# A decoder layer on one core: two transposes moved from TensorE to block-moving DMAs and VectorE

## The chip, the cores and the metric

The kernel runs on one core of a Trainium2 chip. The core has five engines that run side by side, each with its own queue of instructions in a fixed order: TensorE (PE, matrix products), VectorE (DVE), ScalarE (ACT), GpSimd (POOL) and SyncE (SP), which here only issues DMAs. Sixteen DMA engines move the data. PE writes to PSUM, which has eight banks; everything else lies in SBUF, in 128 partitions. The metric is the device time of one execution in microseconds (us), the median of several runs.

## The reference

For four batch entries of 512 rows and 512 columns (f32) it computes a pre-norm decoder layer: causal self-attention with 16 heads of 32 columns, causal cross-attention in which the context serves as keys and as values without any weights, and a feed-forward part with a gated expert. Every part is preceded by a layer norm and added to x.

```python
x = x + attn(_layernorm(x), q_w, q_b, k_w, k_b, v_w, v_b, o_w, o_b)   # softmax(q k^T / sqrt(32)), causal
x = x + _mha(_layernorm(x), ctx_2048, ctx_2048)                       # the same, k = v = context
x = x + ffn(_layernorm(x), W_up, W_down, W_gate, W_expert)            # relu(f Wup) Wdown + sum(rw) * (f Wexpert)
```

In the cross-attention masked scores are set to -10000 and not to minus infinity.

## The kernel before

**Tiling.** The rows of one entry are split into four tiles of 128 rows (`NT`), the columns into four blocks of 128 (`NC`), and a block of 128 columns holds four heads (`HG`). A tensor is kept either by rows (128 rows on the partitions) or turned, with the columns on the partitions: `[128, 4, 512]`, block by row. A projection contracts over columns, so it needs its input turned. This holds for the normalised x of every norm and for the context, which the cross-attention needs both by rows (`cv`, the values) and turned (`ck_t`, the keys).

**How turning is done.** The helper `columns` (line 255) has PE transpose eight 128x128 blocks into a PSUM pair, that is two banks (line 259), and ACT copy the pair to SBUF (line 265, or with a factor at line 267).

**Stages.** The loop at line 1033 goes over the four entries b. Per entry: `with_maxima` runs the score products whose row maxima the softmax needs, with other matmuls between them; `attend` runs the products again, the exponentials and the products with the values; `out_projection` (line 739) multiplies by the output weights; then the norm before the cross-attention, turned by `norm_cross` (line 766, tile `tp_q`); then `with_maxima`, `attend` and `add_cross` for the cross-attention; then the norm, turned by `norm_ffn`, and the feed-forward part. Parts of the feed-forward and of the next entry's projections serve as filling in the `with_maxima` stages.

**What runs ahead.** The next entry's first norm is made inside the current entry's self-attention `with_maxima` (`norm_in(b + 1)`, line 604): tiles `xin` are loaded, and `xn_a` are the normalised tiles, four of them. Its `turns` and those of the context (`context`, line 714) are run by `out_projection` as `sides`, between the groups of matmuls: after the first group the first two tiles of the context and one half of x, after the second group the other half of the context, after the third the other half of x. After the second group stand also the suffix sums of the context on DVE, `behT` (`behind`, line 725, four scans at line 730). At its end the sums `pm_o` are added to x on DVE (line 760), each tile's statistics are taken, and the norm `xn_q` is made (line 216).

**After the output projection** PE's order is: two steps of filling (line 1047; the next entry's query and key projection, `pm_qk`, from `xnT`; in the last entry the gate product and one step of the up projection), then the transposes of `xn_q` tiles 0 and 1 (`tp_q`), one more step, and those of tiles 2 and 3.

**What sets the order.** PE, DVE, ACT and POOL run in the order in which the program issues (`BY_HAND`, line 17). SP's order is set by a scheduler. The framework gives DMAs eight completion lanes in turn, so a DMA is issued only once the eighth before it has landed. Tiles of one tag share a buffer, and a new tile waits until all readers of the old one are done. `xn_t` has one buffer: the turned x of the next entry may be written only after the value projection `pm_v` of the current one, which reads it. For entry 0 that projection stands in the self-attention `with_maxima`; for the later ones it was done in the entry before. The tags `ck_t` and `beh_t` also hold the sums of exponentials of the self-attention's head groups (line 432): group 1 has `beh_t`, groups 0 and 2 have `ck_t`. The sums of group 1 are last read by PE at line 562, the second of three such groups of matmuls in the stage.

Of the kernel before, what the change touches and what calls it, by code (L numbers as in the profile page):

```python
# [9 lines left out]
F32 = mybir.dt.float32  # L10
# [8 lines left out]
P = 128  # L19
# [7 lines left out]
def decoder_layer(  # L27
# [21 lines left out]
    nc = tc.nc  # L49
    B, S, D = x.shape  # L50
    NH = 16
    HD = D // NH
    NT = S // P
    NC = D // P
    HG = P // HD
# [4 lines left out]
    act = ctx.enter_context(tc.tile_pool(name="act", bufs=1))  # L60
# [4 lines left out]
    def pair(name):  # L65

        return ps.tile([P, 2, S], F32, tag="ps", name=name)
# [78 lines left out]
    for r in range(HG):  # L146
# [23 lines left out]
        out=nfloor,  # L170
        in_=nfloor,
# [8 lines left out]
    for n in range(2):  # L180
        t = const.tile([P, NT, P], BF16, name=f"parts{n}")
# [3 lines left out]
    def keep_warm(name, count):  # L185

        out = pair(name)
        for n in range(count):
            nc.tensor.matmul(
                out[:, 0, :P], lhsT=ident, rhs=ident, start=True, stop=True  # L190
            )
# [63 lines left out]
    def columns(srcs, dst, t, tp, scale=None):  # L255

        for n, src in enumerate(srcs):
            for c in range(NC):
                nc.tensor.transpose(
                    tp[:, n, c * P : (c + 1) * P], src[:, c * P : (c + 1) * P], ident  # L260
                )
        to = dst[:, :, t * P : (t + 2) * P].rearrange("p c (n q) -> p c n q", q=P)
        come = tp.rearrange("p n (c q) -> p c n q", q=P)
        if scale is None:
            nc.scalar.copy(to, come)
        else:
            nc.scalar.mul(to, come, scale)
# [336 lines left out]
    def norm_in(b, given=None):  # L604

        e = Entry()
        e.b, e.x, e.xn_t = b, given, None
        src = x[b].rearrange("(t p) d -> p t d", p=P)

        def source(t):  # L610
            if given is not None:
                return given[:, t, :]
            xi = work.tile([P, D], F32, tag="xin", name=f"xin_{b}_{t}")
            nc.sync.dma_start(out=xi, in_=src[:, t, :])
            return xi

        made, norms = layernorms(source, f"a{b}", ahead=given is not None)
        if given is not None:
            norms = [norms[n] for n in (0, 1, NT, NT + 1, 2, 3, NT + 2, NT + 3)]

        def turn(t):
            if e.xn_t is None:
                e.xn_t = act.tile([P, NC, S], F32, tag="xn_t", name=f"xnT_{b}")
            columns(
                [made[t], made[t + 1]],
                e.xn_t,
                t,
                pair(f"tp_a{b}_{t}"),
            )

        def turn_one(t):
            if t == 0:
                e.xn_t = act.tile([P, NC, S], F32, tag="xn_t", name=f"xnT_{b}")
            tp = pair(f"tp_a{b}_{t}")[:, 0, :]
            for c in range(NC):
                cols = slice(c * P, (c + 1) * P)
                nc.tensor.transpose(tp[:, cols], made[t][:, cols], ident)
            nc.scalar.copy(
                e.xn_t[:, :, t * P : (t + 1) * P], tp.rearrange("p (c q) -> p c q", q=P)
            )  # L640

        if given is not None:
            return e, norms, [(lambda t=t: turn_one(t)) for t in range(NT)]
        return e, norms, [(lambda t=t: turn(t)) for t in (0, 2)]

    def add_bias(e):
        for t in range(NT):
            nc.gpsimd.tensor_tensor(e.x[:, t, :], e.x[:, t, :], bo_sb, ALU.add)
# [65 lines left out]
    def context(e):  # L714

        b = e.b
        e.cv = cvs.pop(b)
        e.ck_t = act.tile([P, NC, S], F32, tag="ck_t", name=f"ckT_{b}")

        def one(t):  # L720
            columns([e.cv[:, t, :], e.cv[:, t + 1, :]], e.ck_t, t, pair(f"tp_c{b}_{t}"))

        return [(lambda t=t: one(t)) for t in (0, 2)]

    def behind(e, c):

        if c == 0:
            e.beh_t = act.tile([P, NC, S], F32, tag="beh_t", name=f"behT_{e.b}")
        nc.gpsimd.memset(e.beh_t[:, c, S - 1 : S], 0.0)
        nc.vector.tensor_tensor_scan(  # L730
            e.beh_t[:, c, S - 2 :: -1],
            e.ck_t[:, c, S - 1 : 0 : -1],
            zero.to_broadcast([P, S - 1]),
            0.0,
            ALU.add,
            ALU.add,
        )

    def out_projection(e, a, sides):

        b = e.b
        pms = [pair(f"pm_o{b}_{n}") for n in range(2)]
        for c in range(NC):
            for t in range(NT):
                nc.tensor.matmul(  # L745
                    pms[t // 2][:, t % 2, :],
                    lhsT=a.out[:, c, t * P : (t + 1) * P],
                    rhs=wo_sb[:, c, :],
                    start=(c == 0),
                    stop=(c == NC - 1),  # L750
                )
            if c < NC - 1:
                run(sides[c::3])
            if c == 1:
                for g in range(NC):
                    behind(e, g)

        def add(t):
            xi = e.x[:, t, :]
            nc.vector.tensor_tensor(xi, pms[t // 2][:, t % 2, :], xi, ALU.add)  # L760

        made, norms = layernorms(lambda t: e.x[:, t, :], f"q{b}", add)
        run(norms)
        return made
# [149 lines left out]
    def run(steps):  # L914
        for step in steps:
            for _ in step() or ():
                pass
# [101 lines left out]

    with tc.manual_schedule(engines=BY_HAND):  # L1020
        e, norms, turns = norm_in(0, x0)
        keep_warm("warm", 12)
        between_self = query_key(e) + value(e)
        run(norms[:4] + turns[:2] + between_self[:1])
        run(norms[4:] + turns[2:])
        nc.gpsimd.tensor_scalar(bqs_sb, bq_sb, SCALE, None, ALU.mult)
        nc.vector.tensor_reduce(
            fold, ident.rearrange("p (c e) -> p e c", e=HD), axis=AX.X, op=ALU.add
        )
        add_bias(e)  # L1030
        between_self = between_self[1:]
        skip, between_cross, ahead = 6, [], []
        for b in range(B):
            more = b + 1 < B
            sa = Attention(e.q_t, e.k_t, e.v, False, f"s{b}")
            norms, turns = [], []
            if more:
                after, norms, turns = norm_in(b + 1)
            late = with_maxima(between_self, sa, skip, norms)
            if b == B - 1:  # L1040
                e.x = load_x(b)
            attend(sa, late)
            if b > 0:
                add_bias(e)
            made = out_projection(e, sa, context(e) + turns)
            steps = (query_key(after) if more else []) + between_cross
            run(steps[:2])
            norm_cross(e, made, 0)
            run(steps[2:3])
            norm_cross(e, made, 2)  # L1050
            ca = Attention(e.cq_t, e.ck_t, e.cv, True, f"c{b}")
            ca.e, ca.out = e, e.beh_t
            late = with_maxima(steps[3:], ca)
            if b + 2 < B:
                after.x = load_x(b + 1)
            attend(ca, late)
            if more:
                cvs[b + 1] = load_cv(b + 1)
            filler = value(after) if more else ahead
            run(filler[:1])  # L1060
            made = add_cross(e, ca)

            fill = matmuls(filler[1:])
            for t, k in ((0, 8), (2, 2)) if b != B - 2 else ((0, 12), (2, 0)):
                for _ in range(k):
                    next(fill)
                norm_ffn(e, made, t)
            for _ in fill:
                pass
            gates, ups, downs, experts = ffn(e)  # L1070
            if b + 3 < B:
                between_self, between_cross = gates[:1] + ups + gates[1:] + downs, experts
            elif b + 2 < B:
                between_self, between_cross = gates[:1] + ups + gates[1:] + downs, []
                ahead = experts
            elif more:
                between_self, ahead = ahead + ups[:2], experts
                between_cross = gates[:1] + ups[2:] + gates[1:] + downs
            else:
                run(gates[:1] + ups + gates[1:])  # L1080
                run(downs[:2] + experts[:2] + downs[2:] + experts[2:])
            skip = 0
            if more:
                e = after
# [48 lines left out]
```

## Time and profile before

| | |
|---|---|
| Median of 3 runs | 802.95 us (802.95 to 803.22) |
| Profiled execution's own time | 803.28 us |
| Its span, first to last instruction | 801.5 us |
| PE busy | 794.1 us (99%) |
| DVE busy | 566.4 us (71%) |
| ACT busy | 395.4 us (49%) |
| POOL busy | 340.0 us (42%) |
| DMA packets | 16337, of them 2064 under 512 B |
| TensorE clock granted | 1.0 throughout |

The profiled execution is 0.33 us above the median, and 1.8 us of it lie outside the span. Busy is the time in which an engine had at least one instruction in work. Matmuls overlap: the duration of one (272 ns for a 128x128 f32 transpose) runs from its start to its result, while the next may start long before. What a matmul costs PE is the distance to the next one's start. One 128x512 f32 matmul appears as two instructions.

### The profile page before, as it was taken

To read this page: it belongs to the slowest core of one execution; us is meant where nothing else is said; L and a number is where in the kernel's file an instruction comes from. 1 tells how busy PE (TensorE), PEld (TensorE's weight loads), DVE (VectorE), ACT (ScalarE), POOL (GpSimd) and SP (SyncE) were. 2 spreads that over 40 slices of the span, in tenths; PEclk is the share of its full clock that TensorE was granted. 3 is DMA by queue.
4 is the path that set the end of the run, shared out by engine and by line. 5 is a ranking of instruction groups with operands and counts; after the bars stand their busy time and mean duration, and the time that the engine had idled before them with its cause. 6 is when DMAs were issued, how large, how long until landed. Compare 5 with 4: busy or idle time off the path is not lost.

```text
span 801.5 us, 13955 instructions
## 1 busy us (share of the span) xinstructions
PE 794.1 (99%) x5600; PEld 379.5 (47%) x5600; DVE 566.4 (71%) x963; ACT 395.4 (49%) x450; POOL 340.0 (42%) x523
## 2 busy tenths in 40 slices
PE   8999999999999999999999999999999999999998
PEld 7444554445444454444544445444444454444444
DVE  2478866888678854588867786688859766988512
ACT  2557426871547515666045752687056824674110
POOL 3435612664234732267233482266423653475100
PEclk9999999999999999999999999999999999999999
DMA  9700000001000000021100000000102000000101
GB/s 311 266 28 1 2 1 1 2 28 54 1 27 1 2 1 0 2 80 53 53 14 14 1 2 1 0 1 2 54 28 80 2 2 0 1 2 2 52 1 52
DMA packets 16337, 24.51 MB, mean 31 GB/s; under 512 B 2064, under 2 KB 6416, under 8 KB 16272
## 3 DMA queue, kind: packets, MB, share of 16 engines
q1 hardware_dynamic: 15552, 22.96, 8.3%
q8 instruction: 44, 0.72, 0.4%
q10 hardware_dynamic: 720, 0.66, 0.2%
q14 instruction: 21, 0.17, 0.1%
HBM read 19.42 MB, written 4.19 MB: 29 GB/s over the span
## 4 chain that ended last, share of the span: by engine, by line
PE 96%; ACT 2%; issue 1%; DVE 0%; POOL 0%; POOLq 0%
PE pm_qk L245 13%; PE pm_d L233 7%; PE pm_u L245 7%; PE pm_v L233 7%; PE pm_o L745 7%; PE pm_e L233 7%; PE pv_c L486 6%; PE pv_s L486 6%; PE sm_c L297 6%; PE sm_s L297 6%; PE sc_s L409 5%; PE sc_c L409 5%; PE sc_s L420 1%; PE sc_c L420 1%; PE pv_s L562 1%
## 5 line engine op out<-in xcount | busy, mean ns | idle before, releaser
L328 DVE TENSOR_REDUCE nm_s<-s_s 128x2 f32<-128x1024 f32 (+3 forms) x128 | 96.9, 810 | 31.0 <-POOL s_s L316 30.9
L328 DVE TENSOR_REDUCE nm_c<-s_c 128x2 f32<-128x1024 f32 (+3 forms) x128 | 95.9, 811 | 31.0 <-POOL s_c L316 31.0
L308 ACT COPY s_s<-sm_s 128x1024 f32<-128x1024 f32 x80 | 77.1, 1015 | 70.7 <-PE sm_s L297 36.4
L308 ACT COPY s_c<-sm_c 128x1024 f32<-128x1024 f32 x80 | 77.1, 1016 | 35.9 <-PE sm_c L297 16.2
L316 POOL TENSOR_SCALAR_AFFINE_SELECT s_c<-s_c 128x512 f32<-128x512 f32 (+1 forms) x80 | 44.1, 552 | 100.2 <-ACT s_c L308 100.2
L316 POOL TENSOR_SCALAR_AFFINE_SELECT s_s<-s_s 128x512 f32<-128x512 f32 (+1 forms) x80 | 44.0, 554 | 92.9 <-ACT s_s L308 92.9
L556 DVE TENSOR_TENSOR sum_s<-sum_s,pt_s 128x256 f32<-128x256 f32 (+2 forms) x72 | 60.0, 898 | 15.4 <-PE pv_s L486 15.4
L443 ACT ACTIVATE pt_c<-sc_c 128x1024 f32<-128x1024 f32 x64 | 61.7, 1031 | 18.4 <-PE sc_c L420 10.1
L233 PE MATMUL pm_d<-wdown_sb,hT 128*128 128x512 f32 x128 | 61.5, 610 | 0.0
L451 POOL TENSOR_SCALAR_AFFINE_SELECT pt_c<-pt_c 128x512 f32<-128x512 f32 (+1 forms) x64 | 52.5, 828 | 21.1 <-ACT pt_c L443 20.7
L245 PE MATMUL pm_u<-fT,wup_sb 128*128 128x512 f32 x128 | 59.3, 604 | 0.0
L443 ACT ACTIVATE pt_s<-sc_s 128x1024 f32<-128x1024 f32 x56 | 53.9, 1029 | 10.5 <-POOL pt_s L451 5.5
L233 PE MATMUL pm_v<-wv_sb,xnT 128*128 128x512 f32 x128 | 58.8, 600 | 0.0
L745 PE MATMUL pm_o<-wo_sb,oT_s 128*128 128x512 f32 x128 | 57.8, 596 | 0.0
L409 PE MATMUL sc_c<-cqT,ckT 32*128 32x384 f32 (+3 forms) x512 | 56.4, 464 | 0.9 <-ACT sum_c L443 0.9
L245 PE MATMUL pm_qk<-xnT,wk_sb 128*128 128x512 f32 x120 | 57.3, 607 | 0.0
L245 PE MATMUL pm_qk<-xnT,wq_sb 128*128 128x512 f32 x120 | 56.7, 604 | 0.0
L233 PE MATMUL pm_e<-wexp_sb,fT 128*128 128x512 f32 x120 | 56.3, 604 | 0.0
L451 POOL TENSOR_SCALAR_AFFINE_SELECT pt_s<-pt_s 128x512 f32<-128x512 f32 (+1 forms) x56 | 48.0, 867 | 16.8 <-ACT pt_s L443 16.2
L409 PE MATMUL sc_s<-qT,kT 32*128 32x128 f32 (+3 forms) x512 | 54.0, 464 | 0.9 <-ACT sum_s L443 0.9
L297 PE MATMUL sm_c<-ckT,cqT 32*128 32x512 f32 (+3 forms) x512 | 47.5, 460 | 0.0
L297 PE MATMUL sm_s<-kT,qT 32*128 32x512 f32 (+3 forms) x512 | 47.0, 461 | 0.0
(177 smaller groups left out, 1274.8 us busy)
## 6 DMA issues: line engine op xcount, KB each, us to landing
cv<-in_ctx_dram SPq DMA_DIRECT2D x16, 256.0 KB, 3.7
out_dram<-x SPq DMA_DIRECT2D x15, 256.0 KB, 2.1
xin<-in_x_dram SPq DMA_DIRECT2D x12, 256.0 KB, 2.6
x<-in_x_dram SPq DMA_DIRECT2D x12, 256.0 KB, 4.0
wv_sb<-in_wv_dram SPq DMA_DIRECT2D x1, 1024.0 KB, 8.3
wo_sb<-in_wo_dram SPq DMA_DIRECT2D x1, 1024.0 KB, 9.9
wup_sb<-in_wup_dram SPq DMA_DIRECT2D x1, 1024.0 KB, 9.9
wdown_sb<-in_wdown_dram SPq DMA_DIRECT2D x1, 1024.0 KB, 12.1
```

The lines of the kernel that those rows point to most:

```text
L233: nc.tensor.matmul(pm, lhsT=lhs_t[:, c, t * P : (t + 1) * P], rhs=w[:, c, :], start=(c == 0), stop=(c == NC - 1),)
L245: nc.tensor.matmul(pm, lhsT=w[:, c, f * P : (f + 1) * P], rhs=rhs_t[:, c, :], start=(c == 0), stop=(c == NC - 1),)
L297: nc.tensor.matmul(scs[r // 2][:, r % 2, c : c + (i + 1) * P], lhsT=self.q_t[h, g, i * P : (i + 1) * P], rhs=self.k_t[h, g, : (i + 1) * P] ...
L308: nc.scalar.copy(s, scs[n])
L316: nc.gpsimd.affine_select(out=diagonal, in_=diagonal, compare_op=ALU.is_ge, fill=NEG, base=0, pattern=[[0, 2], [0, len(pieces)], [-1, P]], ...
L328: nc.vector.tensor_reduce(self.nm[g][:, i, 2 * n : 2 * n + 2], made[n][:, :, c : c + (i + 1) * P], axis=AX.X, op=ALU.max, negate=True,)
L409: nc.tensor.matmul(scs[r // 2][:, r % 2, c : c + S - j * P], lhsT=self.k_t[h, g, j * P : (j + 1) * P], rhs=self.q_t[h, g, j * P :], start= ...
L443: nc.scalar.activation(pt, scs[n], AF.Exp)
L451: nc.gpsimd.affine_select(out=diagonal, in_=diagonal, compare_op=ALU.is_ge, fill=0.0, base=0, pattern=[[0, 2], [0, len(pieces)], [1, P]], ...
L486: nc.tensor.matmul(pv[r * HD : (r + 1) * HD, u, j * P :], lhsT=ones if u else self.v[:, j, h * HD : (h + 1) * HD], rhs=pts[r // 2][:, r % ...
L556: nc.vector.tensor_tensor(to, to, pts[n][:, :, c : c + S - j * P], ALU.add)
L745: nc.tensor.matmul(pms[t // 2][:, t % 2, :], lhsT=a.out[:, c, t * P : (t + 1) * P], rhs=wo_sb[:, c, :], start=(c == 0), stop=(c == NC - 1),)
```

## The change

The context, and the normalised x of entries 1 to 3, are no longer turned on PE. A 128x128 transpose is split in two: moving 32x32 blocks to their transposed places, and transposing each block within itself. DMAs from SBUF to SBUF do the first: 32 partitions at a time, in runs of 32 f32 (128 B). DVE's transpose, which turns 32x32 blocks within themselves, does the second.

For x, `move` issues 64 DMAs of 16 KB per entry (128 runs each) straight into `xn_t`, after `with_maxima` in program order, and DVE turns the blocks in place in four instructions of 128x512. For the context, 16 DMAs of 64 KB per entry (512 runs each) go to a tile `cp` that has the tag `beh_t`, and DVE turns from there into `ck_t`, also in four instructions. Over the whole kernel 112 PE transposes, 14 ACT copies and 14 PSUM pairs go, and 256 DMAs and 28 DVE transposes come. The eight DVE transposes of an entry stand between the last product of the self-attention (line 525) and the scans (line 730), those of x first. Entry 0's x is turned on PE as before. On SP the DMAs of a tile of `xn_a` stand behind the `xin` load that waits for the same or the next tile; those of the context follow those of x.

```diff
@@ norm_in
-        def turn(t):
-            if e.xn_t is None:
-                e.xn_t = act.tile([P, NC, S], F32, tag="xn_t", name=f"xnT_{b}")
-            columns(
-                [made[t], made[t + 1]],
-                e.xn_t,
-                t,
-                pair(f"tp_a{b}_{t}"),
-            )
+        def move():
+            e.xn_t = act.tile([P, NC, S], F32, tag="xn_t", name=f"xnT_{b}")
+            for t in range(NT):
+                for i in range(HG):
+                    for j in range(HG):
+                        s = t * P + j * HD
+                        nc.sync.dma_start(
+                            out=e.xn_t[i * HD : (i + 1) * HD, :, s : s + HD],
+                            in_=made[t][j * HD : (j + 1) * HD].rearrange(
+                                "p (c i q) -> p i c q", i=HG, q=HD
+                            )[:, i],
+                        )
+
+        def turn(c):
+            nc.vector.transpose(e.xn_t[:, c, :], e.xn_t[:, c, :])
...
-        return e, norms, [(lambda t=t: turn(t)) for t in (0, 2)]
+        e.move = move
+        return e, norms, [(lambda c=c: turn(c)) for c in range(NC)]
@@ context
         e.cv = cvs.pop(b)
+        cp = act.tile([P, HG, NT * NC, HD], F32, tag="beh_t", name=f"cp_{b}")
+        for i in range(HG):
+            for j in range(HG):
+                nc.sync.dma_start(
+                    out=cp[i * HD : (i + 1) * HD, j],
+                    in_=e.cv[j * HD : (j + 1) * HD].rearrange(
+                        "p t (c i q) -> p i (t c) q", i=HG, q=HD
+                    )[:, i],
+                )
+        come = cp.rearrange("p j (t c) q -> p c t j q", c=NC)
         e.ck_t = act.tile([P, NC, S], F32, tag="ck_t", name=f"ckT_{b}")
 
-        def one(t):
-            columns([e.cv[:, t, :], e.cv[:, t + 1, :]], e.ck_t, t, pair(f"tp_c{b}_{t}"))
-
-        return [(lambda t=t: one(t)) for t in (0, 2)]
+        def one(c):
+            nc.vector.transpose(
+                e.ck_t[:, c, :].rearrange("p (t j q) -> p t j q", j=HG, q=HD), come[:, c]
+            )
+
+        return [(lambda c=c: one(c)) for c in range(NC)]
@@ out_projection
-            if c < NC - 1:
-                run(sides[c::3])
+            if c < 2:
+                run(sides[c * NC : (c + 1) * NC])
@@ the loop over entries
             late = with_maxima(between_self, sa, skip, norms)
+            if more:
+                after.move()
             if b == B - 1:
                 e.x = load_x(b)
             attend(sa, late)
             if b > 0:
                 add_bias(e)
-            made = out_projection(e, sa, context(e) + turns)
+            made = out_projection(e, sa, turns + context(e))
```

## The prediction

> **What bounds the kernel now.** I read the page first, then the waits of PE, then the stretch around entry 0's output projection on PE and DVE in order of time, then SP's DMA issues.
>
> ```profile
> span 801.5 us, 13955 instructions
> PE 794.1 (99%) x5600; PEld 379.5 (47%) x5600; DVE 566.4 (71%) x963; ACT 395.4 (49%) x450; POOL 340.0 (42%) x523
> PE 96%; ACT 2%; issue 1%; DVE 0%; POOL 0%; POOLq 0%
> ```
>
> The first line is the span, the second the busy times, the third the chain that ended last. PE is 96% of that chain, and its waits of all kinds in the list of waits add up to 4.0 us. So PE's stream of matmuls sets the time: a matmul taken out shortens it, unless PE then waits for the others. Here is the stretch on PE (start, duration, engine, line, output and inputs, count):
>
> ```profile
> 94.60 3.70 PE L745 MATMUL pm_o<-wo_sb,oT_s 128*128 128x512 f32 x8
> 98.14 1.04 PE L259 MATMUL tp_c<-ident,cv 128*128 128x128 f32 x8
> 99.01 1.04 PE L259 MATMUL tp_a<-ident,xn_a 128*128 128x128 f32 x8
> 99.88 3.60 PE L745 MATMUL pm_o<-wo_sb,oT_s 128*128 128x512 f32 x8
> 103.32 1.04 PE L259 MATMUL tp_c<-ident,cv 128*128 128x128 f32 x8
> 104.19 3.60 PE L745 MATMUL pm_o<-wo_sb,oT_s 128*128 128x512 f32 x8
> 107.63 1.04 PE L259 MATMUL tp_a<-ident,xn_a 128*128 128x128 f32 x8
> 108.50 3.60 PE L745 MATMUL pm_o<-wo_sb,oT_s 128*128 128x512 f32 x8
> 111.94 3.60 PE L245 MATMUL pm_qk<-xnT,wq_sb 128*128 128x512 f32 x8
> 115.37 3.60 PE L245 MATMUL pm_qk<-xnT,wk_sb 128*128 128x512 f32 x8
> 118.80 1.04 PE L259 MATMUL tp_q<-ident,xn_q 128*128 128x128 f32 x8
> ```
>
> Starts count: eight transposes take PE 0.87 us (103.32 to 104.19), a group of pm_o 3.44 us (99.88 to 103.32). The transposes stand bare in the stream. DVE in the same stretch:
>
> ```profile
> 96.59 0.69 DVE L525 TENSOR_TENSOR oT_s<-pv_s,dt_s 128x512 f32<-128x512 f32 x1
> 105.44 4.56 DVE L730 TENSOR_TENSOR_SCAN behT<-ckT,zero 128x511 f32<-128x511 f32 x4 [8.16 <-ACT ckT L265]
> 110.42 0.69 DVE L760 TENSOR_TENSOR x<-pm_o,x 128x512 f32<-128x512 f32 x1 [0.42 <-PE pm_o L745]
> 115.47 0.52 DVE L216 TENSOR_SCALAR xn_q<-x,mv_q,rs_q 128x512 f32<-128x512 f32 x1
> ```
>
> DVE is idle for 8.16 us just where the change puts its transposes. From the first add to x (110.42) to the end of the second norm tile (115.99) it takes 5.57 us, and PE asks for that tile at 118.80: 2.8 us of slack.
>
> **What goes.** Entries 0 to 2 lose four groups of eight transposes each, entry 3 two: 14 x 0.87 = 12.2 us of PE. The 14 ACT copies (1.01 us each) go from an engine busy 49% of the time, worth nothing on the path.
>
> **What DVE gets.** Its 128x512 f32 transpose has a row:
>
> ```profile
> L586 DVE STREAM_TRANSPOSE dt_s<-rden_s x16: 711/711/712, 85.0 to 649.9; 128x512 f32<-128x512 f32 x16
> ```
>
> Eight cost 5.7 us in entries 0 to 2, four 2.8 us in entry 3; the strided input of the context's may cost up to a scan's 1.2 us each. Cover: line 525 ends at 97.28, the transposes by 103.0, the scans by 107.5. PE, no longer interrupted, runs pm_o from 94.60 to 108.4 and has the first half at about 106.9. The adds start 0.6 us late, and 2.1 us of slack remain. POOL's memsets of behT now wait for DVE; behind them stand only the statistics, which DVE feeds later still. So DVE costs nothing if its data have landed. If not, scans, adds and norms queue behind the waiting transposes, PE waits at tp_q, and the 2.1 us are all the cover.
>
> **The Trainium skill against it.** By those rows TensorE turns 512x512 in 1.74 us and DVE in 2.84 us plus DMAs; what decides is that DVE idles there. The Trainium skill, "VectorE: DVE Perf Modes", section "Rules for kernel authors", says to transpose 128x128 on TensorE if the PSUM destination is fine; taken as a rule this would mean no gain, and the rows agree on raw cost only.
>
> **What the DMAs cost.** Per entry SP issues 64 for x (128 runs each; not in entry 3), then 16 for the context (512 runs). Eight may be in flight. No row has SBUF-to-SBUF traffic or runs of 128 B, so I bound it by SP's loads (start, length of the group, count):
>
> ```profile
> 4.52 0.51 SPq L109 DMA_DIRECT2D wq_sb<-in_wq_dram  x1
> 5.07 0.51 SPq L109 DMA_DIRECT2D wk_sb<-in_wk_dram  x1
> 17.50 1.62 SPq L130 DMA_DIRECT2D wgate_sb<-in_wgate_dram  x1
> 19.16 2.53 SPq L91 DMA_DIRECT2D wexp_sb<-in_wexp_dram  x1
> ...
> 186.15 2.11 SPq L86 DMA_DIRECT2D cv<-in_ctx_dram  x4
> 357.76 1.76 SPq L75 DMA_DIRECT2D x<-in_x_dram  x4
> ```
>
> A DMA of 128 runs is spaced 0.44 us (1.76/4); the median issue of xin, 0.33 us, is the low end, 0.55 us the high one. A DMA of 512 runs: wq to wk, with four times the bytes, 0.55 us (4.52 to 5.07); low 0.33; high 1.66 us, wgate to wexp (17.50 to 19.16), 512 runs of 32 B into a full queue. I take 0.44 for x, and for the context 0.55, wq being nearest in run count without wgate's backlog. Landing after the last issue: 2.5 us, near xin's median of 2.6.
>
> The Trainium skill, "DMA: Bandwidth & Descriptors", section "Rules for kernel authors", says that transfers under 64 KB are mostly overhead and should be coalesced; its section "Anatomy of one DMA" puts about 2 us on each. My estimate from that figure, one after another, is 128 us for entry 0's 64, slower by far; eight in flight make it 0.25 us each, under the issue. The rows (0.44 us apart) show them overlapping; for these small runs none does.
>
> **Are they in time?** Call u the price of a context DMA. The rest from the landing to tp_q's data is 2.84 + 4.56 + 5.57 = 12.97 us.
>
> Entry 0: xnT is free only when pm_v ends at 64.48. 64 x 0.44 = 28.2 brings SP to 92.7, the context's 16 x 0.55 = 8.8 to 101.5, landed at 104.0. DVE is ready for it at 100.1. tp_q's data come at 117.0; PE asks at 94.60 + 4 x 3.44 + 6.86 = 115.2. PE waits 1.8 us: in general 16u - 7.1.
>
> Entries 1 and 2: xnT is long free, so x's DMAs follow each tile's norm; the last norm (250.84) is 27 us ahead of pm_o. The context must wait for line 562's second group, the last reader of beh_t (268.40): landed at 268.4 + 8.8 + 2.5 = 279.7, while DVE is busy till 283.4. No wait; in general 16u - 14.6.
>
> Entry 3: from 639.16, landed at 650.5, before DVE ends line 525 (651.30). Slack at tp_q is small here: the norm tile at 668.60, PE at 668.83. But the scans end by 658.7 and the first half of pm_o comes 1.74 us earlier, at 661.3: no wait; in general 16u - 12.5.
>
> SP's later loads and stores start far from here. An xin load behind 16 of x's DMAs (7 us) keeps its time: its norm tiles are 14 us apart in entry 1 (219.95, 234.15).
>
> Sum: 803.28 - 12.2 + 1.8 = 792.9 us for the profiled execution; 0.33 less against the median: **792.6 us**.
>
> **The rivals.**
> 1. The context's DMAs throttle: runs of 128 B cost the DMA engines more than issuing costs SP. The four waits (entry 0's counts from u = 0.44, entry 3's from 0.78, the others' from 0.91) eat the 12.2 us at u = 0.95, and beyond it the kernel is slower. At wgate's 1.66: 19.5 + 2 x 12.0 + 14.1 = 57.6, so 848 us; at 1.2: 12.1 + 2 x 4.6 + 6.7 = 28, so 819. For it: wgate's row, and 32 partitions a time instead of 128. Against: wgate stood in a queue full of weights, and here no other traffic runs.
> 2. x's issue is at its high end, 0.55: entry 0 alone loses 64 x 0.11 = 7.0 more, 799.6 us. For it: wq's spacing. Against: those carry 512 runs.
> 3. All hidden: x at 0.33 ends entry 0's moves at 85.6, the context lands at 96.9, no wait: 790.7 us.
> 4. DVE ends last: the context's transposes at 1.2 us put the scans 2.0 us later, inside the 2.1 of entries 0 to 2; in entry 3 inside its margin of 2.6. Hardly a loss; it stacks with 1 or 2.
>
> That the change doesn't do what it says is excluded: the built program holds no tp_c, and tp_a in entry 0 alone.
>
> **How the numbers follow.** Chances: forecast 0.38, rival 1 0.40 (0.36 of it slower, 0.04 about even), rival 2 0.14, rival 3 with 4 0.08. So faster by over 0.2% (about what a measurement of this kernel tells from no change) 0.60, within it 0.04, slower 0.36. The forecast's own range is 790 to 797 us. For eight in ten the range must reach into rival 1: from 789.5, a little under the full gain, to 822, u near 1.2; above it lies some 0.16.
>
> **What would show it.** Right: pm_o's groups follow each other at 3.44 us; the waits of PE at tp_q are near 2 us in entry 0 and zero in the others; DVE's idle time before the first transpose of ckT is near 4 us in entry 0 and zero elsewhere; x's DMAs are spaced 0.44 us, the context's 0.55. Wrong: context DMAs spaced over 0.95 us, with DVE waiting for cp in every entry, or x's DMAs spaced wider than 0.5 us, with SP the latest in entry 0.

## The result, and the profile after

The changed kernel takes 811.5 us (median of 4 runs, 811.04 to 812.89), the kernel before 802.96: a ratio of 1.0109, 95% interval 1.0096 to 1.0121. It is 1% slower. The forecast was 792.6 us and faster; the measured time lies inside the stated range, on the other side of the kernel before.

The page of the changed kernel, span, busy times, the clock that TensorE was granted in 40 slices, and the chain that ended last by engine:

```profile
span 811.2 us, 14123 instructions
PE 787.4 (97%) x5488; PEld 369.6 (46%) x5488; DVE 584.1 (72%) x991; ACT 381.6 (47%) x436; POOL 339.1 (42%) x523
PEclk9999995999999999999999999999999999999999
PE 89%; SPq 4%; DVE 2%; ACT 2%; issue 2%; DMA 0%; POOL 0%; DVEq 0%; POOLq 0%
```

SP's queue, which issues DMAs, is on the chain for the first time with 4%, PE fell from 96% to 89%, and one slice of forty, the one around 130 us, has a lower clock. All three point to one place. Here is entry 0's output projection on PE (start, duration, engine, line, output and inputs, count, and in brackets the idle time before with what ended it):

```profile
94.68 14.00 PE L764 MATMUL pm_o<-wo_sb,oT_s 128*128 128x512 f32 x32
112.07 5.37 PE L245 MATMUL pm_qk<-xnT,wq_sb 128*128 128x512 f32 x8 [3.38 <-DMA cp<-cv]
117.27 3.60 PE L245 MATMUL pm_qk<-xnT,wk_sb 128*128 128x512 f32 x8
133.13 1.09 PE L259 MATMUL tp_q<-ident,xn_q 128*128 128x128 f32 x4 [12.26 <-DVE xn_q L216]
135.01 1.11 PE L259 MATMUL tp_q<-ident,xn_q 128*128 128x128 f32 x4 [0.80 <-DVE xn_q L216]
135.92 5.80 PE L245 MATMUL pm_qk<-xnT,wq_sb 128*128 128x512 f32 x8
141.56 1.04 PE L259 MATMUL tp_q<-ident,xn_q 128*128 128x128 f32 x8
142.52 1.15 PE L297 MATMUL sm_c<-ckT,cqT 32*128 32x256 f32 x16
```

The groups of pm_o now follow each other without a break, as wanted. Then PE waits 3.4 us, 12.3 us and 0.8 us, and two projections that should take 3.44 us from start to start take 5.20 and 5.64: the granted clock was 0.50 from 114 to 116 us and from 133 to 139. The view puts the wait of 3.4 us down to the context's DMAs; but pm_qk reads xnT, which DVE began to turn at 111.26, so it was x that came late. On SP and on DVE in the same stretch stands why:

```profile
64.65 45.10 SPq L627 DMA_DIRECT2D xnT<-xn_a  x64
109.93 10.69 SPq L728 DMA_DIRECT2D cp<-cv  x16
```

```profile
96.68 0.69 DVE L525 TENSOR_TENSOR oT_s<-pv_s,dt_s 128x512 f32<-128x512 f32 x1
111.26 2.49 DVE L635 STREAM_TRANSPOSE xnT<-xnT 128x512 f32<-128x512 f32 x4 [13.89 <-DMA xnT<-xn_a]
122.42 2.49 DVE L738 STREAM_TRANSPOSE ckT<-cp 128x512 f32<-128x512 f32 x4 [8.67 <-DMA cp<-cv]
124.94 4.56 DVE L749 TENSOR_TENSOR_SCAN behT<-ckT,zero 128x511 f32<-128x511 f32 x4
129.42 0.66 DVE L779 TENSOR_TENSOR x<-pm_o,x 128x512 f32<-128x512 f32 x1
```

SP takes 45.1 us for 64 DMAs of 16 KB, 0.705 us each, then 0.67 us for each of the context's 16. The DMA engines were busy 0.16 of the time in the first of these stretches, so they did not hold SP back; nor did the eight completion lanes, since eight issues of 0.60 us take 4.8 us and a DMA of x lands 1.8 us after its issue (median, 3.9 at most). DVE waits 13.9 us for the first and 8.7 us for the second; the adds to x start at 129.4, long after pm_o.

In entries 1 and 2 the same work is in time. Entry 2, on PE and then on DVE:

```profile
489.74 14.00 PE L764 MATMUL pm_o<-wo_sb,oT_s 128*128 128x512 f32 x32
503.58 3.60 PE L245 MATMUL pm_qk<-xnT,wq_sb 128*128 128x512 f32 x8
507.01 3.60 PE L245 MATMUL pm_qk<-xnT,wk_sb 128*128 128x512 f32 x8
510.44 1.04 PE L259 MATMUL tp_q<-ident,xn_q 128*128 128x128 f32 x8
```

```profile
494.75 2.45 DVE L738 STREAM_TRANSPOSE ckT<-cp 128x512 f32<-128x512 f32 x4
497.23 4.56 DVE L749 TENSOR_TENSOR_SCAN behT<-ckT,zero 128x511 f32<-128x511 f32 x4
502.13 0.69 DVE L779 TENSOR_TENSOR x<-pm_o,x 128x512 f32<-128x512 f32 x1 [0.34 <-PE pm_o L764]
```

For comparison the kernel before: the first sm_c of entry 0, then pm_o and the first tp_q of entry 2:

```profile
124.08 1.15 PE L297 MATMUL sm_c<-ckT,cqT 32*128 32x256 f32 x16
...
474.83 3.70 PE L745 MATMUL pm_o<-wo_sb,oT_s 128*128 128x512 f32 x8
...
499.03 1.04 PE L259 MATMUL tp_q<-ident,xn_q 128*128 128x128 f32 x8
```

The balance by starts on PE: from pm_o to the first tp_q entry 1 went from 24.20 to 20.71 us, entry 2 from 24.20 to 20.70, entry 3 from 20.22 to 18.46, together 8.75 us less. Entry 0, from pm_o to the first sm_c, went from 29.48 to 47.84, 18.36 us more. The difference, 9.61, is the span's growth (811.2 - 801.5 = 9.7). So the change does all it should in three entries and loses it twice over in one.

### The profile page after: what moved, and what is told of

It reads as the page before. It is cut to its first block, busy times and chain, and to the rows that moved or that the text cites. A ratio compares the mean times of both kernels' runs of the same rounds, so it can differ in the third digit from the quotient of the medians.

```text
span 811.2 us, 14123 instructions
## 1 busy us (share of the span) xinstructions
PE 787.4 (97%) x5488; PEld 369.6 (46%) x5488; DVE 584.1 (72%) x991; ACT 381.6 (47%) x436; POOL 339.1 (42%) x523
## 4 chain that ended last, share of the span: by engine, by line
PE 89%; SPq 4%; DVE 2%; ACT 2%; issue 2%; DMA 0%; POOL 0%; DVEq 0%; POOLq 0%
PE pm_qk L245 12%; PE pm_d L233 7%; PE pm_u L245 7%; PE pm_v L233 7%; PE pm_e L233 7%; PE pv_c L486 6%; PE sm_c L297 6%; PE sm_s L297 5%; PE pm_o L764 5%; PE sc_c L409 5%; PE pv_s L486 5%; PE sc_s L409 4%; SPq L627 3%; PE sc_s L420 1%; SPq L728 1%
## 5 line engine op out<-in xcount | busy, mean ns | idle before, releaser
L245 PE MATMUL pm_qk<-xnT,wq_sb 128*128 128x512 f32 x120 | 60.7, 641 | 3.4 <-DMA cp<-cv 3.4
L764 PE MATMUL pm_o<-wo_sb,oT_s 128*128 128x512 f32 x128 | 56.0, 595 | 0.0
L671 ACT ACTIVATE kT<-pm_qk,bk_sb 128x512 f32<-128x512 f32 x16 | 11.0, 688 | 90.6 <-PE pm_qk L245 86.0
```

The costliest lines, as they stand in the source:

```text
L245: nc.tensor.matmul(pm, lhsT=w[:, c, f * P : (f + 1) * P], rhs=rhs_t[:, c, :], start=(c == 0), stop=(c == NC - 1),)
L764: nc.tensor.matmul(pms[t // 2][:, t % 2, :], lhsT=a.out[:, c, t * P : (t + 1) * P], rhs=wo_sb[:, c, :], start=(c == 0), stop=(c == NC - 1),)
```

## The experiments

Theory Q, the queue: x's DMAs of entry 0 may start only when pm_v has read xnT (64.6 us), each holds SP for 0.70 us, 64 of them take until 110, and the context's stand behind. Its rival C puts the loss on the context's DMAs.

**The context alone.** x goes back to PE.

```diff
-        e.move = move
-        return e, norms, [(lambda c=c: turn(c)) for c in range(NC)]
+        e.move = lambda: None
+        return e, norms, [(lambda t=t: turn_pe(t)) for t in (0, 2)]   # the old turn, through PE and ACT
```

> Only the context is turned by DMAs and VectorE; x is turned by TensorE as before. Theory Q (the queue): the loss is entry 0's 64 x DMAs on SP, about 0.70 us each, which start only when pm_v has read xnT (64.6 us) and push the context's DMAs behind them. Without them the context's 16 start at 85 us, land near 98, DVE needs them at 97.3, and the 8 groups of transposes (8 x 0.87 = 7.0 us) are a pure gain: 796.0 us, no wait of TensorE at tp_q. Rival C (the context): its DMAs, held back by the buffer of the sums and by their own price, are late by themselves; then TensorE still waits at tp_q in entry 0, and the time is 800 us or more.

Measured: 796.19 us, ratio 0.9916 (0.9900 to 0.9933). On SP in entry 0, then the waits of PE in the whole kernel:

```profile
85.44 11.72 SPq L735 DMA_DIRECT2D cp<-cv  x16
```

```profile
PE warm L189 <- POOL ident masks.py:199: 1.5, 1, 1.5
PE sc_c L409 <- ACT sum_c L443: 0.9, 4, 0.2
PE sc_s L409 <- ACT sum_s L443: 0.9, 4, 0.2
PE pm_qk L695 <- ACT xnT L649: 0.7, 1, 0.7
```

The 16 DMAs start when the sums' buffer is free and end at 97.2. DVE still waits 1.5 us for them, but PE never waits at tp_q. Rival C falls.

**Entry 1's x alone back on PE.** This is the one that is turned inside entry 0; x of entries 2 and 3 and the context stay with DMAs.

```diff
+        if b == 1:
+            e.move = lambda: None
+            return e, norms, [(lambda t=t: turn_pe(t)) for t in (0, 2)]
         e.move = move
```

> As the changed kernel, but entry 1's x, the one that is turned inside entry 0, is turned by TensorE. Theory Q: no x DMAs stand ahead of entry 0's context any more, so the whole wait goes, and with it the halved TensorE clock after it: 12.2 - 2 x 0.87 = 10.4 us under the kernel before, 792.5 us. Rival C: entry 0 still waits for the context's DMAs, 800 us or more.

Measured: 792.5 us, ratio 0.9869 (0.9855 to 0.9884), no wait of PE at tp_q. One quarter of the DMAs, 64 of 256, carried the whole loss.

**Another buffer.** All 256 DMAs stay; only two tags are exchanged.

```diff
-            e.xn_t = act.tile([P, NC, S], F32, tag="xn_t", name=f"xnT_{b}")   # in move
+            e.xn_t = act.tile([P, NC, S], F32, tag="f_t", name=f"xnT_{b}")
...
-                [P, NC, S], F32, tag="f_t" if b != B - 2 else "xn_t", name=f"fT_{b}"
+                [P, NC, S], F32, tag="xn_t" if b != B - 2 else "f_t", name=f"fT_{b}"
...
-                    [P, NC, S], F32, tag="o_t" if b != B - 2 else "f_t", name=f"hT_{b}"
+                    [P, NC, S], F32, tag="o_t" if b != B - 2 else "xn_t", name=f"hT_{b}"
```

> As the changed kernel with all 256 DMAs, but the turned x of entries 1 to 3 lies in the buffer of the tag f_t, and the feed-forward tiles that lay there lie in xn_t; no more SBUF is used. Then the first x DMAs of entry 0 need not wait for pm_v and can start when the first norm tile is made, near 41 us. Theory Q (the start is what is late, the price of 0.70 us is the same): x's DMAs are done by 67.6 + 16 x 0.7 = 79 us, the context lands near 98, no wait, full gain of 12.2 us: 790.8 us. Rival S (these DMAs ahead of the xin loads on SP, or beside the scores, cost as much as they save): the norm tiles of entry 0 come late, VectorE waits for xin, and the time stays above 797 us.

Measured: 790.75 us (790.71 to 790.79), ratio 0.9847 (0.9833 to 0.9862). SP in entry 0:

```profile
42.36 11.43 SPq L627 DMA_DIRECT2D xnT<-xn_a  x16
53.88 0.53 SPq L614 DMA_DIRECT2D xin<-in_x_dram  x1
54.46 32.61 SPq L627 DMA_DIRECT2D xnT<-xn_a  x48
87.25 11.65 SPq L728 DMA_DIRECT2D cp<-cv  x16
```

The price is the same (11.43/16 = 0.71 us), only the start is 22 us earlier. x ends at 87.1, not at 79 as expected, since SP works through the tiles without a pause from 54.5 on; the context comes 2 us later than it could, and PE still never waits at tp_q. Rival S falls. This version beats both kernels by its whole interval.

**x alone.** The context goes back to PE.

```diff
-        cp = act.tile([P, HG, NT * NC, HD], F32, tag="beh_t", name=f"cp_{b}")
...
+        def one(t):
+            columns([e.cv[:, t, :], e.cv[:, t + 1, :]], e.ck_t, t, pair(f"tp_c{b}_{t}"))
+
+        return [(lambda t=t: one(t)) for t in (0, 2)]
```

> Only x is turned by DMAs and VectorE; the context is turned by TensorE as before. Theory Q: entry 0's 64 x DMAs run from 64.6 to about 110 on SP and land at 111.5; VectorE turns until 114, the scans end at 118.6, the norm tile that tp_q needs comes at 124.2, and TensorE could have asked for it at 117.0: some 7 us lost against a gain of 6 x 0.87 = 5.2 us, 805 us, 804 to 807 with a lower TensorE clock after the wait. So this part alone loses a little, and the full change loses more because the context's 16 DMAs stand behind the 64. Rival C (the context's DMAs are the cause): the gain of 5.2 us, 797.8 us.

Measured: 805.46 us (804.03 to 806.15), ratio 1.0028 (1.0017 to 1.0040). SP issues the 64 from 64.47 to 108.51, DVE turns at 110.0, and PE waits 2.6 and 0.8 us at tp_q. So x's part loses alone, the context's part wins alone (6.8 us), and together they lose more than x alone, because the context's DMAs stand behind x's on SP.

**Fewer DMAs, the same bytes and the same start.** In entry 0 the four norm tiles of entry 1 lie in one tile; 16 DMAs of 64 KB go to the buffer of the tag xn_t, and DVE turns from there into f_t. It is built on the version with exchanged tags.

```diff
+        if b == 1:
+            joint = act.tile([P, NT, D], F32, tag="f_t", name="xn_joint")
...
+            if joint is not None:
+                cpx = act.tile([P, HG, NT * NC, HD], F32, tag="xn_t", name="cpx")
+                for i in range(HG):
+                    for j in range(HG):
+                        nc.sync.dma_start(
+                            out=cpx[i * HD : (i + 1) * HD, j],
+                            in_=joint[j * HD : (j + 1) * HD].rearrange(
+                                "p t (c i q) -> p i (t c) q", i=HG, q=HD
+                            )[:, i],
+                        )
```

> In entry 0 the four norm tiles of entry 1 lie in one tile, and the blocks of x are moved by 16 DMAs of 64 KB instead of 64 of 16 KB: the same bytes, the same runs of 128 B, to the same buffer xn_t and so with the same earliest start after pm_v; VectorE then turns from there into another buffer. Entries 1 and 2 keep 64 DMAs. Theory Q with a price for each DMA whatever its size: 16 x 0.67 = 10.7 us from 67.7, done by 79, the context lands near 98, no wait, 790.8 us. Rival V (bytes or runs set the price, or the late start alone is the cause): x's DMAs still end after 100 us, TensorE waits, 803 us or more.

Measured: 790.89 us, ratio 0.9848 (0.9831 to 0.9864).

```profile
67.66 11.81 SPq L632 DMA_DIRECT2D cpx<-xn_joint  x16
85.22 11.53 SPq L752 DMA_DIRECT2D cp<-cv  x16
```

The same megabyte in the same runs of 128 B takes 11.8 us instead of 45.1. So SP pays per DMA here, not per byte or run. Rival V falls. A start after pm_v is early enough if there are 16.

**What sets the price of a DMA.** The forecast had taken 0.44 us from loads of x. Two kernels add DMAs to the kernel before, in a stretch where SP is idle; nothing reads what they write.

```diff
+        for k in range(8):     # 32 partitions, 4 runs of 128 B, SBUF to another quadrant
+            nc.sync.dma_start(out=t[quads[0], :, s], in_=blocks(v[quads[1], k % NT]))
...
+        for k in range(4):     # 128 partitions, one run of 512 B, SBUF to SBUF
+            nc.sync.dma_start(out=t[:, k, 3 * P :], in_=v[:, k, :P])
...
```

> The kernel before, with 40 DMAs on SP more, issued in entry 0's self-attention into a buffer that is free there; the output does not use them. Forms: blocks of 32 partitions with 4 runs of 128 B each from SBUF to another quadrant of SBUF (as the change does), one run of 512 B per partition over 32 partitions, blocks within one quadrant, 128 partitions with 4 runs of 128 B, 128 partitions with one run of 512 B, and 32 partitions with 4 runs of 128 B from DRAM. What sets the issue time of about 0.60 us? Theory E (both ends in SBUF): all five SBUF forms near 0.60, the DRAM form 0.33 to 0.45. Theory P (32 partitions instead of 128): the three forms of 32 partitions from SBUF and the DRAM form near 0.60, the two of 128 partitions 0.33 to 0.45. Theory R (the pattern of short runs): the forms with 4 runs near 0.60, those with one run 0.33 to 0.45. The time itself is to stay near 803 us, since SP is idle there.

Measured in one execution (issue time min/median/max in ns, in the order of the expectation; `...` stands for lines left out):

```profile
L1029 SPq DMA_DIRECT2D probe<-v x8: 599/603/1535, 56.0 to 72.3; - x8
...
L1032 SPq DMA_DIRECT2D probe<-v x8: 588/589/597, 58.8 to 74.8; - x8
...
L1035 SPq DMA_DIRECT2D probe<-v x8: 599/606/633, 61.3 to 77.4; - x8
...
L1038 SPq DMA_DIRECT2D probe<-v x4: 638/657/690, 63.9 to 78.8; - x4
...
L1040 SPq DMA_DIRECT2D probe<-v x4: 599/618/636, 65.3 to 80.2; - x4
...
L1043 SPq DMA_DIRECT2D probe<-in_ctx_dram x8: 597/612/1352, 66.7 to 83.5; - x8
```

All six stand near 0.60 us; the time, 803.58 us, shows that SP was idle there. That refutes each theory as written: E had the DRAM form at 0.33 to 0.45, P the two of 128 partitions, R those with one run. So a second kernel separated the length of the run, the number of partitions and the source.

```diff
+        for k in range(NC):    # 128 partitions, one run of 2 KB, SBUF to SBUF; then the same from DRAM
+            nc.sync.dma_start(out=t[:, k, :], in_=v[:, k, :])
+        for k in range(NC):
+            nc.sync.dma_start(out=t[:, k, :], in_=rows[k])
...
```

> A second look at the issue time, since in the first every form took about 0.60 us, from DRAM too: the kernel before with 24 other DMAs. Forms: 128 partitions with one run of 2 KB from SBUF to SBUF, the same from DRAM (as the loads of x), 32 partitions with one run of 2 KB from DRAM, 128 partitions with 4 runs of 128 B from DRAM, 128 partitions with one run of 512 B from DRAM, 32 partitions with one run of 2 KB from SBUF to SBUF. Theory SH (short runs): the forms with runs of 128 B and 512 B near 0.60, all forms with 2 KB 0.33 to 0.45. Theory E or P (both ends in SBUF, or fewer than 128 partitions, each for itself): from DRAM over 128 partitions 0.33 to 0.45 whatever the run, the other three near 0.60.

Measured, again in that order:

```profile
L1028 SPq DMA_DIRECT2D probe<-v x4: 471/576/593, 56.0 to 66.2; - x4
...
L1030 SPq DMA_DIRECT2D probe<-in_ctx_dram x4: 333/343/352, 58.4 to 68.7; - x4
...
L1032 SPq DMA_DIRECT2D probe<-in_ctx_dram x4: 311/327/340, 61.1 to 73.3; - x4
...
L1034 SPq DMA_DIRECT2D probe<-in_ctx_dram x4: 630/632/632, 75.2 to 77.2; - x4
...
L1036 SPq DMA_DIRECT2D probe<-in_ctx_dram x4: 355/433/1092, 80.1 to 82.1; - x4
...
L1038 SPq DMA_DIRECT2D probe<-v x4: 588/590/597, 82.6 to 84.5; - x4
```

This kernel took 803.63 us, also one execution; there are four issues of each form, and those of 512 B spread widely (355 to 1092 ns). Neither theory holds alone. From SBUF to SBUF the median is 0.58 to 0.59 us even for 2 KB rows over all partitions. From DRAM it is 0.33 to 0.34 with 2 KB rows, over 32 partitions as well as 128, 0.43 with 512 B, and 0.63 with 128 B. Either of two things, both ends in SBUF or runs of 128 B, brings the price to about 0.6; the moving DMAs have both and cost no more for it. The number of partitions plays no part that shows here. Why is open. So is why a long row averages 0.705 us when the median issue is 0.599: single issues of up to 1.80 us and short gaps between issues make up the rest.

**The clock.** TensorE idles 12.3 us in entry 0. Here idle matmuls fill it, between the two steps of filling and tp_q: 52, and in the second kernel 64.

```diff
             run(steps[:2])
+            if b == 0:
+                keep_warm("warm_0", 52)
             norm_cross(e, made, 0)
```

> The changed kernel with 52 matmuls of 128x128 that nobody reads, in entry 0 between the two steps of filling and the first transposes of tp_q, where TensorE waits 12.3 us; they take about 11 us at the full clock, so they should not lengthen the wait. Theory K (part of the loss is the granted clock of 0.5 that follows the wait): the query projection behind tp_q goes in 3.4 us instead of 5.6 and the transposes at the full rate; about 2.7 us less than the changed kernel, 808.8 us. Rival (the lower clock is hidden under waits that end at the same time anyway): no change, 811.5 us, or more if the idle matmuls lengthen the stretch.

Measured: 812.29 us (812.11 to 812.9), no gain. They ended at 129.7, and the 2.9 us that were left were enough: the granted clock was 0.64 in the stretch from 133 to 142.5 us, and the query projection took 5.53 us from start to start.

> As the kernel with 52 idle matmuls in entry 0, with 64 of them: at the measured 0.226 us for each they end near 132.4 us, so that TensorE waits under 1 us before the first transposes of tp_q instead of 2.9 us, where the clock still fell. Theory K (the halved clock that follows a gap of more than about 2.6 us is part of the loss): the clock stays at 1.0 behind tp_q, the query projection takes 3.4 us instead of 5.6, and the time is 2 to 3 us under that of the 52, near 809.5 us. Rival (the clock falls for another reason, or the waits hide it): 812 us.

Measured: 810.12 us (median of 5, 809.88 to 811.36), 2.2 us less than with 52. The end of the wait in both kernels, first with 52, then with 64:

```profile
132.67 0.91 PE L259 MATMUL tp_q<-ident,xn_q 128*128 128x128 f32 x4 [2.93 <-DVE xn_q L216]
134.65 1.11 PE L259 MATMUL tp_q<-ident,xn_q 128*128 128x128 f32 x4 [1.07 <-DVE xn_q L216]
135.55 5.69 PE L245 MATMUL pm_qk<-xnT,wq_sb 128*128 128x512 f32 x8
```

```profile
134.75 0.60 PE L259 MATMUL tp_q<-ident,xn_q 128*128 128x128 f32 x4
135.85 0.66 PE L259 MATMUL tp_q<-ident,xn_q 128*128 128x128 f32 x4 [0.51 <-DVE xn_q L216]
136.45 3.70 PE L245 MATMUL pm_qk<-xnT,wq_sb 128*128 128x512 f32 x8
```

With 64 the clock stayed at 1.0 behind the wait and the projection took 3.54 us instead of 5.53. But tp_q began 0.9 us after its data were there (133.8): in this execution the first gap, 3.4 us, had halved the clock ahead of the idle matmuls, and they started later. So the executions that these lines show differ by only 1.1 us (811.36 with 64, 812.46 with 52), the medians by 2.2; every time with 64 lies below every time with 52. The clock after the wait thus accounts for 1 to 2 us of the loss, and the rest is the wait.

## Why the prediction was wrong

**What goes** held: 14 groups of transposes at 0.87 us. The version with exchanged tags, where PE never waits at tp_q, is 12.25 us under its kernel before (803.0 to 790.75), against 12.2 in the sum.

**What DVE gets** held. Four transposes take 2.49 us, 0.62 each against the 0.71 taken, and the strided input costs nothing. Where the data are in time, DVE is no bound.

**What the DMAs cost** is the step that failed, in the price of x's DMAs: 0.44 us taken, 0.55 as the high end, 0.705 measured. Over 64 that is 17.0 us more. The context's u was taken as 0.55 and measured as 0.67 (0.69 to 0.78 in the later entries): 1.9 us more. With both, the formula for entry 0 gives 1.8 + 17.0 + 1.9 = 20.7 us of loss; the trace shows 21.8, the 18.36 that entry 0 grew by and the 3.48 of the four groups of transposes that it no longer has. The clock was in no term (the projection behind the wait took 5.64 us instead of 3.44); faster transposes on DVE give a part back. The rows that bounded the price were loads from DRAM with runs of 2 KB and 512 B. I had said that no row shows SBUF-to-SBUF traffic, and still took the ends from one kind of row; wgate, whose 1.66 us I used for the context alone, should have widened x's price too.

**Are they in time** was right in its mechanism: entry 0 is the tight one, because xnT is free only at 64.5 us, and in entries 1 to 3 PE never waits at tp_q. It was nearly right on the landing (2.5 us taken, 2.3 measured for the context). At the measured price entry 1 had little room left: x's DMAs ended at 285.40, and the context's could start at 286.92. In entry 3 the context landed after DVE was ready, not before it as forecast; DVE waited 0.74 us, and the formula at the measured u of 0.69 (16u - 12.5) is still below zero, so PE did not.

**The rivals.** The slower side was given to the context's DMAs throttling from u = 0.95. That did not happen: u = 0.67, and the context alone is a gain. What happened is rival 2, x's issue, with a price beyond its stated end; it is also the second sign of being wrong that the prediction names (x's DMAs wider apart than 0.5 us, SP the latest in entry 0). Entry 0's loss, 1.8 + 64 x (price - 0.44), reaches the 12.2 us of gain at 0.60. Rival 2's 0.14 stood wholly on the faster side. That the measured time lies inside the stated range is luck: the range reached up to 822 us for rival 1, which did not occur. Rival 3, all hidden, is what two of the experiments made true.

**The Trainium skill against it.** The rule of "VectorE: DVE Perf Modes", "Rules for kernel authors", that a 128x128 transpose belongs on TensorE, would have kept the kernel before, and against the change as made it was right in its outcome. Against the version with exchanged tags it was wrong by 1.5%: where PE is the bound and DVE idles, the dearer path is the faster one. The rule of "DMA: Bandwidth & Descriptors", "Rules for kernel authors", to coalesce transfers under 64 KB, was the one to weigh more: 64 DMAs of 16 KB cost 45.1 us of SP, 16 of 64 KB cost 11.8. The fixed 2 us of its section "Anatomy of one DMA", which that section gives for DMAs issued from GpSimd while SP issues these, did not add up one after another, as the prediction said: a DMA of x lands 1.8 us after its issue (median), and the next is issued 0.705 us after it. What added up was the issue.

## What to carry to other kernels

Price a new kind of DMA by its issue on the queue that issues it, and count: 64 x 0.7 us is a stage's length, while the bytes (1 MB) were never the question. When many small DMAs must be in time, look first at what lets them start, often only the buffer they write to: exchanging two tags turned a loss of 1.1% into a gain of 1.5%, and one DMA for four did the same. If a price has no row, let the far ends widen every term that uses it.

## What was not expected of the hardware

- SP's issue of a DMA takes about 0.6 us when both ends lie in SBUF (0.58 to 0.66 in all seven such forms) and when the runs from DRAM are 128 B (0.61 to 0.63), 0.33 to 0.34 with 2 KB rows from DRAM. The moves of the context, 512 runs of 128 B each, issue in 0.63 us, those of x with 128 runs in 0.60.
- A gap of TensorE halved the granted clock after 3.4 us (0.50 from 114 to 116 us in the changed kernel), after 2.9 us (52 idle matmuls, 0.50 from 133.1 us on) and, with x alone, after 2.6 us (0.50 from 120.5 us on, when a second gap of 0.8 us was still to come; the projection behind took 5.39 us). Another gap of 2.6 us, in the kernel with 52 idle matmuls, left it at 1.00 from 111 to 118 us. So near this length the length alone did not decide. The Trainium skill, "TensorE: Matmul & The Clock Gate", "Why this matters for your kernels", sets about 3 us as the limit; one gap shorter than that halved the clock here.
